# Spiking recommender scores on one core: four more table parts held before the score stage, an opening in two-part chunks, and a plainer last step

## The chip, the cores and the metric

The kernel runs on one core of a Trainium2 chip. The metric is device time in microseconds (us), the median over several executions; one further execution was profiled. Engines are named as in the profile: PE is TensorE (matmul; PEld is its weight load), DVE is VectorE, ACT is ScalarE, POOL is GpSimd, SP is SyncE, which here only issues DMAs. A line such as L478 is a line of the kernel before.

## The reference

```
B, T, D, N = 1024, 50, 128, 100001
e      = emb[seq]                        # row 0 of the table is zero
prefix = cumsum(e, axis=1)
uF     = prefix / minimum(t + 1, lengths)
y      = (uF - mean(uF)) * rsqrt(var(uF) + 1e-5) * gamma + beta    # over the batch, per step
for t in range(T):                       # integrate and fire
    v = v + (y[:, t] - v) / 2
    spike[t] = v >= 1
    v = v - spike[t]
scores = spike.mean(over t) @ emb.T      # 1024 x 100001, f32
```

The inputs are 1024 sequences of 50 indices, their lengths, a table of 100001 rows of 128 f32 values (51 MB), gamma and beta. The output has 409.6 MB.

## The kernel before

**Step stage.** Everything is held with D = 128 on the partitions and the batch of 1024 along the free axis. For each of the 50 steps POOL issues eight indirect DMAs (`gather`, 128 table rows each) into a tile `e`; PE transposes the eight blocks of 128 rows and adds them into two PSUM tiles `pre`, which so hold the running sum. DVE scales them into `uF` and takes the batch statistics (`bn_stats`, `bn_aggr`), ACT takes the square root and centres `uF`, DVE makes the factor `a` out of a few 128x1 operations, ACT writes `x` into the PSUM tile `v`, and DVE applies the old state (`negv`, which is spike minus v) in `step`. PE sums the spikes of every step into `sums` (`counted`). After the last step the spike counts lie in `countA`, `countB` and `countC`, for 128, 512 and 384 of the batch.

In the last step the kernel before cuts the batch into three pieces instead of two halves. The block of 128 that is gathered last (`order.append(order.pop(NB // 2))`) is a piece of its own, so that only a 128-wide `uF` and a 128-wide `bn_stats` follow the last gather. `negv` is formed in three parts (`negated`, `thirds`), placed between the operations of the chain.

**Table parts.** The table is cut into 98 parts of 1024 rows (512 KB each; the last has 673 rows). A part passes through three places. `fetch` brings its rows into a slot of a tile `rows` (six parts to a tile, 24 KB per partition). `prepare` transposes them on PE (eight transposes into PSUM), ACT rounds them to `hi`, DVE subtracts to get `lo`; this pair (8 KB per partition) comes from the list `free`. `product` multiplies a pair with one block of 128 counts: four matmuls of 512 columns per part and block.

36 parts (`AHEAD * GROUP`) are fetched by SP at the start of the step stage and stay in SBUF until used. Two of them are split into pairs during the step stage, at t = 42 and t = 46, which leaves their two row slots empty. When the parts of rows0 have been split, its six slots become three more pairs (`places`), and so do those of rows1. rows2 and rows3 later serve as output tiles. Parts from 36 on are fetched by ACT, three at a time, into rows4 and rows5, from chunk MIDDLE on.

**Score stage.** `WIDTHS` lists how many parts each chunk has. For each chunk and each of eight blocks `n` of 128 batch rows, PE makes the products of the chunk's parts, DVE and ACT in turn scale them from PSUM (four tiles of 1024 columns) into an output tile `o`, and SP stores it with one DMA of 128 rows, each as long as the chunk is wide (4 KB for each part). Output tiles come from the list `turns` in rotation. Before, it has four tiles of two parts for chunks 0 to 2, three of three parts for chunks 3 to 6, and three of six parts from chunk 7 on. The pools of the first two phases are closed and their space is used again. While a chunk is computed, `ready` splits the parts of the next one, at blocks 2 to 7, when a pair is free.

| chunks | before | after |
|---|---|---|
| two parts (8 KB rows) | 0 to 2, parts 0 to 5 | 0 to 10, parts 0 to 21 |
| three parts (12 KB rows) | 3 to 6, parts 6 to 17 | none at the start |
| six parts (24 KB rows) | 7 to 18, parts 18 to 89 | 11 to 21, parts 22 to 87 |
| rest | 4, 4 (the last short) | 4, 3, 3 (the last short) |

Order on each engine is program order (`manual_schedule`). SP waits in that order too: for the output tile's evictions, and for the completion semaphore that a store is given. The stores and ACT's fetches share eight such semaphores in turn, and a DMA is issued only when the previous one on its semaphore has landed.

Of the kernel before, what the change touches and what calls it, by code (L numbers as in the profile page):

```python
# [18 lines left out]
ALU = mybir.AluOpType  # L19
# [8 lines left out]
AHEAD = 6  # L28

WIDTHS = [2, 2, 2, 3, 3, 3, 3] + 12 * [6] + [4, 4]  # L30
NARROW, MIDDLE = 3, 7
# [3 lines left out]
def rec_kernel(  # L35
# [19 lines left out]
    embp = ctx.enter_context(tc.tile_pool(name="embT", bufs=1))  # L55

# [25 lines left out]

    def group(g):
        at = g if g < AHEAD else AHEAD - 2 + g % 2
        r = rowp.tile([P, GROUP, HALF], F32, tag=f"rows{at}", name=f"rows_{g}")
        for k in range(GROUP):
            rows[g * GROUP + k] = r[:, k, :]
        return r

    def fetch(r, q, n):  # L90

        engine = nc.sync if q < AHEAD * GROUP else nc.scalar
        k = q % GROUP
# [67 lines left out]
    with ExitStack() as ph:  # L161
# [3 lines left out]
        up = ph.enter_context(tc.tile_pool(name="uF", bufs=2))  # L165
# [13 lines left out]
        for g in range(AHEAD):  # L179
            fetch(group(g), g * GROUP, GROUP)  # L180
# [3 lines left out]
        def gather(t):  # L184
            es[t] = gp.tile([P, B], F32, tag="e", name=f"e_{t}")
            order = list(range(NB))
            if t == T - 1:
                order.append(order.pop(NB // 2))
            for n in order:
                nc.gpsimd.indirect_dma_start(  # L190
                    out=es[t][:, n * P : (n + 1) * P],
                    out_offset=None,
                    in_=table,
                    in_offset=bass.IndirectOffsetOnAxis(ap=idx[:, n, t : t + 1].bitcast(U32), axis=0),
                )
# [84 lines left out]

        thirds = [slice(0, P), slice(P, P + BANK), slice(P + BANK, B)]

        def negated(cs):
            nc.vector.tensor_tensor(negv[:, cs], s[:, cs], v[:, cs], ALU.subtract)

# [6 lines left out]
        for t in range(T):  # L292
# [4 lines left out]
            if last:  # L297
                s = lp.tile([P, B], BF16, tag="s", name=f"s_{t - 1}")
                nc.vector.tensor_single_scalar(s, v, V_TH, ALU.is_ge)
            uF = up.tile([P, B], F32, tag="uF", name=f"uF_{t}")  # L300


            pieces = halves if not last else halves[:1] + [slice(B - 3 * P, B), slice(BANK, BANK + P)]
            bs = sp.tile([P, len(pieces), 6], F32, tag="bs", name=f"bs_{t}")
            for j, cs in enumerate(pieces):
                h = cs.start // BANK
                if last and j == len(pieces) - 1:

                    counted(t - 1, s)
                for c0 in range(cs.start, cs.stop, P):  # L310
                    k = c0 - h * BANK
                    nc.tensor.matmul(  # L312
                        pre[h][:, k : k + P],
                        lhsT=e[:, c0 : c0 + P],
# [6 lines left out]
                nc.vector.scalar_tensor_tensor(  # L321
                    uF[:, cs],
                    rlen[:, cs],
                    1.0 / (t + 1),
                    pre[h][:, cs.start - h * BANK : cs.stop - h * BANK],
                    ALU.max,
                    ALU.mult,
                )
                nc.vector.bn_stats(bs[:, j, :], uF[:, cs])  # L329
            if not last:  # L330
                correct(t + 1, l)
            else:
                count = once.tile([P, B], F32, tag="zT", name="count")
# [8 lines left out]
            ve = sp.tile([P, 1], F32, tag="ve", name=f"ve_{t}")  # L342
            nc.vector.tensor_scalar_add(ve, mv[:, 1:2], BN_EPS)
# [8 lines left out]
            if last:  # L352
                negated(thirds[0])
            nc.vector.reciprocal(r, r)
            q = sp.tile([P, 1], F32, tag="q", name=f"q_{t}")
            nc.vector.scalar_tensor_tensor(q, r, ve, r, ALU.mult, ALU.mult)
# [11 lines left out]
            if not last:  # L368
                vt = vp.tile([P, B], F32, tag=f"v{t % 2}", name=f"v_{t}")
                x(vt, whole)  # L370
                if t:
                    negated(whole)
# [5 lines left out]
                if t in (T - 8, T - 6):  # L378
                    q = (t - T + 8) // 2
                    prepare(q, vp.tile([P, HALF], F32, tag="v1", name=f"pt_{q}"))  # L380

# [3 lines left out]
        warm = vp.tile([P, HALF], F32, tag="v1", name="warm")  # L385
# [3 lines left out]
        groups = list(zip(thirds, (pre[0][:, :P], pre[1], vC), (countA, countB, countC)))  # L389
        negated(thirds[1])  # L390
# [5 lines left out]
        negated(thirds[2])  # L396
# [29 lines left out]
    to_fetch = AHEAD * GROUP  # L426
# [5 lines left out]
    for c, W in enumerate(WIDTHS):  # L432

        if c in (0, NARROW, MIDDLE):
            opening.close()
            where = opening if c < MIDDLE else ctx
            op = where.enter_context(tc.tile_pool(name="o", bufs=1, reuse_waits="tile"))
            if c == 0:
                third = [op.tile([P, HALF], F32R, tag=x, name=x) for x in ("hi2", "lo2")]
                free.append(third)  # L440
                turns = [(op, f"o{k}", 2) for k in range(4)]
            elif c == NARROW:
                assert third in free
                free.remove(third)
                turns = [(op, f"o{k}", 3) for k in (2, 0, 1)]
            else:
                fourth = op.tile([P, 4, HALF], F32R, tag="pairs", name="pairs")
                free.extend((fourth[:, k, :], fourth[:, k + 1, :]) for k in (0, 2))
# [5 lines left out]
        def ready():  # L454
            nonlocal to_split
            if to_split < q2 and free:
# [3 lines left out]
                if to_split in (GROUP, 2 * GROUP):  # L460
                    places(to_split // GROUP - 1)

        for n in range(NB):
# [5 lines left out]
            for q in range(q0, q1):  # L469
# [12 lines left out]
                if n == NB - 1:  # L482
                    free.append(split.pop(q))
# [6 lines left out]
            if n in (1, 4) and c >= MIDDLE and to_fetch < parts:  # L490
                g = to_fetch // GROUP
                if to_fetch % GROUP or to_split >= (g - 1) * GROUP:
                    if to_fetch % GROUP == 0:
                        r = group(g)
# [23 lines left out]
```

## Time and profile before

| what | value |
|---|---|
| median of 4 runs (lowest to highest) | 1575.21 us (1574.97 to 1575.61) |
| the profiled execution | 1575.07 us |
| its span, first to last instruction | 1573.3 us |
| PE, DVE, ACT, POOL busy | 73%, 60%, 40%, 24% of the span |
| mean granted TensorE clock | 0.944 |
| HBM read, written | 77.69 MB, 409.60 MB |
| first store of scores issued | 510.25 us |
| last store of scores issued | 1561.21 us |

The span has two stages. Until 510 us POOL is the busiest engine beside DVE, and the DMA engines are nearly idle but for the first 64 us, when the 36 parts arrive. From 510 us on the DMA engines move 400 GB/s and more. The busy shares of the first table are means over both stages and tell little by themselves.

### The profile page before, as it was taken

The page shows a single profiled execution, that of the slowest core. Times are in us where ns is not written, and L with a number is a line of the kernel's source. Part 1 is how long each engine was busy: PE and PEld are TensorE (multiplying, and loading weights), DVE is VectorE, ACT ScalarE, POOL GpSimd, SP SyncE. Part 2 cuts the span into 40 slices and gives each one's busy share as a digit, 9 for nine tenths or more (in the row PEclk, how much of TensorE's full clock was granted, in tenths as well). Part 3 has the DMA queues.
Part 4 walks back from the last instruction along what each step waited for, and adds up shares of the span by engine and source line. Part 5 has one row for each costly group of instructions (what it writes and reads, how often), then busy time and mean ns, then how long its engine had stood idle before and what let it go on. Part 6 is the DMA issues. An engine that isn't in the chain of part 4 may idle for free.

```text
span 1573.3 us, 12572 instructions
## 1 busy us (share of the span) xinstructions
PE 1144.6 (73%) x4548; PEld 820.2 (52%) x4548; DVE 947.2 (60%) x1165; ACT 630.5 (40%) x700; POOL 378.4 (24%) x406
## 2 busy tenths in 40 slices
PE   4555554555555998899887888788788788888885
PEld 2222222222233776677666666666676666666663
DVE  5777777777777665576555455555455445555453
ACT  2322222222233554465444444444444444444342
POOL 7777777777775000000000000000000000000000
PEclk9999999999975999999999999999999999999898
DMA  9611111111111999999999999999999999999898
GB/s 337 249 52 54 52 54 52 54 52 54 52 54 46 397 410 418 422 393 427 429 427 431 427 429 427 424 417 406 435 414 429 421 420 426 406 427 425 382 427 354
DMA packets 53691, 488.14 MB, mean 310 GB/s; under 512 B 11995, under 2 KB 12796, under 8 KB 32380
## 3 DMA queue, kind: packets, MB, share of 16 engines
q1 hardware_dynamic: 31984, 428.77, 64.9%
q0 software_dynamic: 12800, 26.24, 5.7%
q10 hardware_dynamic: 8844, 32.33, 5.1%
q8 instruction: 36, 0.59, 0.1%
q14 instruction: 27, 0.22, 0.0%
HBM read 77.69 MB, written 409.60 MB: 310 GB/s over the span
## 4 chain that ended last, share of the span: by engine, by line
DMA 54%; POOL 18%; PE 10%; issue 9%; ACT 5%; DVE 3%; DVEq 0%; POOLq 0%; ACTq 0%; SPq 0%
DMA scores<-o 49%; POOL e L190 18%; PE po L149 9%; DMA e<-in_L_rec_emb_table,idx 5%; ACT o L478 4%; DVE o L476 2%; ACT pairs L141 0%; PE pre L312 0%; PE pt L119 0%; DVE s L349 0%; DVE pairs L142 0%; PE sums L267 0%; DMA idx<-in_r_seq 0%; DVE bs L329 0%; DVE uF L321 0%
## 5 line engine op out<-in xcount | busy, mean ns | idle before, releaser
L476 DVE TENSOR_SCALAR o<-po 128x1024 f32<-128x1024 f32 x391 | 464.2, 1221 | 354.5 <-DMA scores<-o 313.6
L478 ACT ACTIVATE o<-po 128x1024 f32<-128x1024 f32 (+1 forms) x391 | 388.1, 1018 | 551.1 <-DMA scores<-o 340.1
L190 POOL DMA_INDIRECT e<-in_L_rec_emb_table,idx x400 | 377.7, 944 | 124.2 <-issue 112.2
L149 PE MATMUL po<-pairs,countB 128*128 128x512 f32 x1168 | 312.1, 413 | 65.7 <-ACT o L478 48.8
L149 PEld LDWEIGHTS po<-pairs,countB 128*128 128x128 f32 x1168 | 224.5, 197 | 129.7 <-ACT o L478 63.3
L149 PE MATMUL po<-pairs,countC 128*128 128x512 f32 x876 | 242.0, 423 | 50.6 <-ACT o L478 50.5
L312 PE MATMUL pre<-ident,e 128*128 128x128 f32 x400 | 148.7, 450 | 145.3 <-DMA e<-in_L_rec_emb_table,idx 145.3
L149 PEld LDWEIGHTS po<-pairs,countC 128*128 128x128 f32 x876 | 171.5, 202 | 97.4 <-ACT o L478 61.6
L312 PEld LDWEIGHTS pre<-ident,e 128*128 128x128 f32 x400 | 79.0, 200 | 234.2 <-DMA e<-in_L_rec_emb_table,idx 209.9
L142 DVE TENSOR_TENSOR pairs<-pt,pairs 128x1024 fp32r<-128x1024 f32 (+1 forms) x73 | 88.4, 1217 | 95.4 <-ACT pairs L141 95.2
L341 ACT ACTIVATE r<-mv,eps 128x1 f32<-128x1 f32 x50 | 14.8, 295 | 301.3 <-DVE mv L337 301.3
L321 DVE SCALAR_TENSOR_TENSOR uF<-rlen,pre 128x512 f32<-128x512 f32 (+1 forms) x101 | 68.5, 678 | 103.6 <-PE pre L312 103.6
L119 PE MATMUL pt<-ident,rows 128*128 128x128 f32 x782 | 110.6, 288 | 6.5 <-ACT o L478 2.7
L119 PEld LDWEIGHTS pt<-ident,rows 128*128 128x128 f32 x782 | 99.9, 151 | 26.8 <-issue 8.9
L267 PE MATMUL sums<-s,ident_h 128*128 128x512 bf16 x98 | 49.6, 608 | 72.1 <-DVE s L349 72.1
L149 PE MATMUL po<-hi,countB 128*128 128x512 f32 x200 | 83.1, 416 | 18.9 <-ACT o L478 14.1
L256 PE MATMUL pre<-zT,l 128*128 128x512 f32 x100 | 77.4, 776 | 19.6 <-DVE uF L321 19.5
L149 PE MATMUL po<-lo,countB 128*128 128x512 f32 x200 | 80.3, 402 | 0.0
L141 ACT CAST pairs<-pt 128x1024 fp32r<-128x1024 f32 (+1 forms) x73 | 73.6, 1008 | 14.5 <-PE pt L119 14.2
L149 PE MATMUL po<-pairs,countA 128*128 128x512 f32 (+1 forms) x292 | 72.8, 393 | 7.5 <-ACT o L478 7.5
L363 ACT ACTIVATE v<-uF,hgb,a 128x1024 f32<-128x1024 f32 x49 | 59.2, 1209 | 42.2 <-DVE a L359 42.2
L149 PE MATMUL po<-hi,countC 128*128 128x512 f32 x150 | 63.5, 424 | 14.8 <-ACT o L478 14.8
(75 smaller groups left out, 824.6 us busy)
## 6 DMA issues: line engine op xcount, KB each, us to landing
scores<-o SPq DMA_DIRECT2D x96, 3072.0 KB, 20.2
scores<-o SPq DMA_DIRECT2D x32, 1536.0 KB, 8.9
rows<-in_L_rec_emb_table ACTq DMA_DIRECT2D x20, 1536.0 KB, 29.7
scores<-o SPq DMA_DIRECT2D x22, 1024.0 KB, 8.0
rows<-in_L_rec_emb_table SPq DMA_DIRECT2D x6, 3072.0 KB, 35.1
scores<-o SPq DMA_DIRECT2D x8, 2048.0 KB, 13.1
scores<-o SPq DMA_DIRECT2D x8, 1872.5 KB, 11.3
e<-in_L_rec_emb_table,idx POOLq DMA_INDIRECT x400, 2.5
```

The costliest lines, as they stand in the source:

```text
L119: nc.tensor.transpose(pt[:, k0 : k0 + kw], r[:kw, k0 : k0 + D], ident[:kw, :kw])
L141: nc.scalar.copy(vh, vp)
L142: nc.vector.tensor_tensor(vl, vp, vh.bitcast(F32), ALU.subtract)
L149: nc.tensor.matmul(po[:, :kw], lhsT=counts[n], rhs=part[:, k0 : k0 + kw], start=j == 0, stop=j == 1,)
L190: nc.gpsimd.indirect_dma_start(out=es[t][:, n * P : (n + 1) * P], out_offset=None, in_=table, in_offset=bass.IndirectOffsetOnAxis(ap=idx[: ...
L256: nc.tensor.matmul(pre[h], lhsT=l, rhs=zT[:, h * BANK : (h + 1) * BANK], start=t == 0, stop=False, skip_group_check=True,)
L267: nc.tensor.matmul(sums[h], lhsT=ident_h, rhs=s[:, h * BANK : (h + 1) * BANK], start=t == 0, stop=t == T - 2, skip_group_check=True,)
L312: nc.tensor.matmul(pre[h][:, k : k + P], lhsT=e[:, c0 : c0 + P], rhs=ident, start=False, stop=last, is_transpose=True, skip_group_check=True,)
L321: nc.vector.scalar_tensor_tensor(uF[:, cs], rlen[:, cs], 1.0 / (t + 1), pre[h][:, cs.start - h * BANK : cs.stop - h * BANK], ALU.max, ALU. ...
L363: nc.scalar.activation(vt, uF[:, cs], AF.Identity, bias=hgb[:, 1:2], scale=a)
L476: nc.vector.tensor_scalar_mul(o[:, h0 : h0 + hw], po[:, :hw], 1.0 / T)
L478: nc.scalar.mul(o[:, h0 : h0 + hw], po[:, :hw], 1.0 / T)
```

## The change

Four things are changed.

- **Two parts in rows that come free.** After the parts 0 and 1 are split at t = 42 and t = 46, SP fetches parts 8 and 9 into their slots (`LATE`). The tile `uF` has one buffer instead of two.
- **Two parts in a tile of their own.** A tile `extra` (8 KB per partition) receives parts 2 and 3. From chunk 1 on it is one of four output tiles of two parts, and from chunk MIDDLE on it holds a pair. Chunk 0 has three output tiles. Altogether 40 parts are held (`HELD`), and ACT fetches 58 parts instead of 62. `slot` tells where a part lies.
- **Two-part chunks up to part 22.** `WIDTHS` as in the table above; the phase of three-part chunks at the start is gone. The extra pair `third` is taken out of use when 16 parts are split. Chunk 10 has two parts and splits the six parts of chunk 11.
- **The last step in halves.** Its gathers come in the usual order, the batch is taken in two halves, `negv` is formed in one operation ahead of `uF`, and the spike count of step 48 follows the last transposes. In all steps `ve` is gone: the factor takes one more 128x1 operation (`tensor_mul`) after the reciprocal.

```diff
-WIDTHS = [2, 2, 2, 3, 3, 3, 3] + 12 * [6] + [4, 4]
-NARROW, MIDDLE = 3, 7
+LATE = 2
+EXTRA = 2
+HELD = AHEAD * GROUP + LATE + EXTRA
+
+WIDTHS = 11 * [2] + 11 * [6] + [4, 3, 3]
+MIDDLE = 11
...
+    def slot(q):
+        if q < 2 + EXTRA:
+            return 0, q % 2
+        if q < GROUP + EXTRA:
+            return 0, q - EXTRA
+        q -= LATE + EXTRA
+        return max(q, 0) // GROUP, q % GROUP if q >= GROUP else q - GROUP + LATE
...
-        engine = nc.sync if q < AHEAD * GROUP else nc.scalar
-        k = q % GROUP
+        engine = nc.sync if q < HELD else nc.scalar
+        k = slot(q)[1]
...
-        up = ph.enter_context(tc.tile_pool(name="uF", bufs=2))
+        up = ph.enter_context(tc.tile_pool(name="uF", bufs=1))
...
-        for g in range(AHEAD):
-            fetch(group(g), g * GROUP, GROUP)
+        tiles = [group(g) for g in range(AHEAD)]
+        fetch(tiles[0], 0, 2)
+        extra = rowp.tile([P, EXTRA, HALF], F32, tag="extra", name="extra")
+        fetch(extra, 2, EXTRA)
...
+        fetch(tiles[0], 2 + EXTRA, GROUP - 2)
+        for g in range(1, AHEAD):
+            fetch(tiles[g], g * GROUP + LATE + EXTRA, GROUP)
...
-            if t == T - 1:
-                order.append(order.pop(NB // 2))
...
             if last:
                 s = lp.tile([P, B], BF16, tag="s", name=f"s_{t - 1}")
                 nc.vector.tensor_single_scalar(s, v, V_TH, ALU.is_ge)
+                nc.vector.tensor_tensor(negv, s, v, ALU.subtract)
...
-            pieces = halves if not last else halves[:1] + [slice(B - 3 * P, B), slice(BANK, BANK + P)]
...
-                if last and j == len(pieces) - 1:
-                    counted(t - 1, s)
...
             else:
+                counted(t - 1, s)
                 count = once.tile([P, B], F32, tag="zT", name="count")
...
-            ve = sp.tile([P, 1], F32, tag="ve", name=f"ve_{t}")
-            nc.vector.tensor_scalar_add(ve, mv[:, 1:2], BN_EPS)
...
-            if last:
-                negated(thirds[0])
             nc.vector.reciprocal(r, r)
             q = sp.tile([P, 1], F32, tag="q", name=f"q_{t}")
-            nc.vector.scalar_tensor_tensor(q, r, ve, r, ALU.mult, ALU.mult)
+            nc.vector.tensor_mul(q, r, r)
+            nc.vector.scalar_tensor_tensor(q, mv[:, 1:2], BN_EPS, q, ALU.add, ALU.mult)
...
                     prepare(q, vp.tile([P, HALF], F32, tag="v1", name=f"pt_{q}"))
+                    fetch(tiles[0], GROUP + EXTRA + q, 1)
+                    rows[GROUP + EXTRA + q] = tiles[0][:, q, :]
...
-        warm = vp.tile([P, HALF], F32, tag="v1", name="warm")
+        warm = vp.tile([P, HALF], F32, tag="v0", name="warm")
...
-        negated(thirds[1])
...
-        negated(thirds[2])
...
-    to_fetch = AHEAD * GROUP
+    to_fetch = HELD
...
-        if c in (0, NARROW, MIDDLE):
+        if c in (0, 1, MIDDLE):
             if c == 0:
+                op = opening.enter_context(tc.tile_pool(name="o", bufs=1, reuse_waits="tile"))
...
-                turns = [(op, f"o{k}", 2) for k in range(4)]
-            elif c == NARROW:
-                assert third in free
-                free.remove(third)
-                turns = [(op, f"o{k}", 3) for k in (2, 0, 1)]
+                turns = [(op, f"o{k}", 2) for k in range(3)]
+            elif c == 1:
+                turns = [(rowp, "extra", 2)] + turns
             else:
-                fourth = op.tile([P, 4, HALF], F32R, tag="pairs", name="pairs")
-                free.extend((fourth[:, k, :], fourth[:, k + 1, :]) for k in (0, 2))
+                assert third not in free and third not in split.values()
+                opening.close()
+                op = ctx.enter_context(tc.tile_pool(name="o", bufs=1, reuse_waits="tile"))
+                for pool, tag in ((op, "pair"), (rowp, "extra")):
+                    t = pool.tile([P, 2, HALF], F32R, tag=tag, name=f"pair_{tag}")
+                    free.append((t[:, 0, :], t[:, 1, :]))
                 turns = [(rowp, "rows2", 6), (rowp, "rows3", 6), (op, "o", 6)]
             blocks = 0
...
-                if to_split in (GROUP, 2 * GROUP):
+                if to_split in (GROUP + LATE + EXTRA, 2 * GROUP + LATE + EXTRA):
                     places(to_split // GROUP - 1)
+                    if to_split > 2 * GROUP and third in free:
+                        free.remove(third)
...
-                    free.append(split.pop(q))
+                    pair = split.pop(q)
+                    if pair is not third or to_split < 2 * GROUP + LATE + EXTRA:
+                        free.append(pair)
                     ready()
...
-                g = to_fetch // GROUP
-                if to_fetch % GROUP or to_split >= (g - 1) * GROUP:
-                    if to_fetch % GROUP == 0:
+                g, k = slot(to_fetch)
+                if k or to_split >= (g - 1) * GROUP + LATE + EXTRA:
+                    if k == 0:
```

## The prediction

> **What bounds the kernel now.** I read the page's slices first. In its DMA line the DMA engines are idle while the steps run and full from the fourteenth slice on, where PE is at 8 to 9 tenths: two stages with different limits.
>
> ```profile
> PE   4555554555555998899887888788788788888885
> ...
> DMA  9611111111111999999999999999999999999898
> ...
> DMA 54%; POOL 18%; PE 10%; issue 9%; ACT 5%; DVE 3%; DVEq 0%; POOLq 0%; ACTq 0%; SPq 0%
> ```
>
> The third line is the chain of work that ended last: POOL with its gathers for the steps, then DMA with the stores. So a saving in the score stage counts if it takes bytes or gaps from the DMA engines, and one in the steps only if the last gather is followed sooner. The second view is the table of windows over the score stage (length, busy time of PE, PEld, DVE, ACT, POOL, then PE clock, DMA share, GB/s).
>
> ```profile
> 525.00:565.00 40.00, 37.11 (x176) 28.58 (x174) 26.39 (x22) 21.92 (x22) 0.00 (x0) 1.00 1.01 418
> 565.00:580.00 15.00, 12.11 (x49) 9.32 (x48) 7.26 (x6) 5.78 (x6) 0.00 (x0) 0.89 0.97 403
> 580.00:660.00 80.00, 71.23 (x328) 54.65 (x327) 47.25 (x40) 39.61 (x41) 0.00 (x0) 1.00 1.00 419
> 660.00:690.00 30.00, 27.22 (x136) 20.81 (x134) 19.46 (x17) 17.20 (x18) 0.00 (x0) 1.00 0.99 415
> 690.00:700.00 10.00, 9.62 (x42) 7.99 (x43) 7.95 (x8) 5.46 (x6) 0.00 (x0) 1.00 0.82 343
> ...
> 760.00:1440.00 680.00, 559.80 (x2431) 440.75 (x2432) 359.26 (x304) 299.41 (x304) 0.00 (x0) 0.93 1.00 423
> ...
> 1460.00:1480.00 20.00, 17.12 (x71) 13.48 (x70) 8.97 (x9) 8.22 (x9) 0.00 (x0) 0.91 0.79 336
> 1480.00:1560.00 80.00, 63.27 (x273) 48.98 (x271) 40.77 (x38) 31.71 (x36) 0.00 (x0) 0.96 1.01 425
> ```
>
> The share is 1.0 in all but three: two-part chunks (first row) move 418 GB/s, three-part 419, six-part with fetches 423. The gaps are the passage to three parts (565 to 580), that to six (690 to 700), and one at 1460 to 1480. The third view, SP's waits from 1430 to 1490 (total, times, longest), names the last; the page's DMA issues have the fetch it waits for.
>
> ```profile
> SPq L158 <- DMA rows<-in_L_rec_emb_table: 14.1, 1, 14.1
> ```
>
> ```profile
> rows<-in_L_rec_emb_table ACTq DMA_DIRECT2D x1, 320.0 KB, 46.7
> ```
>
> A store had the same completion semaphore as the 320 KB fetch of the last part (issued at 1428.8, 46.7 us to landing) and waited for it. Fourth, the timeline at the last step:
>
> ```profile
> 498.96 1.21 DVE L284 TENSOR_TENSOR negv<-s,v 128x1024 f32<-128x1024 bf16 x1
> ...
> 501.64 1.22 DVE L299 TENSOR_SCALAR s<-v 128x1024 bf16<-128x1024 f32 x1
> ...
> 502.78 0.68 DVE L321 SCALAR_TENSOR_TENSOR uF<-rlen,pre 128x512 f32<-128x512 f32 x1
> 503.50 0.69 DVE L329 BATCH_NORM_STATS2 bs<-uF 128x6 f32<-128x512 f32 x1
> ...
> 505.33 0.29 DVE L321 SCALAR_TENSOR_TENSOR uF<-rlen,pre 128x128 f32<-128x128 f32 x1
> 505.65 0.29 DVE L329 BATCH_NORM_STATS2 bs<-uF 128x6 f32<-128x128 f32 x1
> 505.98 0.24 DVE L337 BATCH_NORM_AGGREGATE mv<-bs 128x2 f32<-128x18 f32 x1
> ```
>
> The last gather lands at about 504.7; behind it come only the 128-wide pair and the aggregate, done at 506.22. The rest of the chain leads to the first store at 510.25.
>
> **The change part by part.** The sum is made against the profiled execution, 1575.07 us (span 1573.3 and 1.8 around it), 0.14 under the median of 1575.21.
>
> *Fewer reads in the full stage.* Four parts of 0.524 MB, 2.10 MB, leave a stage that moves 423 GB/s: 2.10 / 0.423 = 4.96 us. **-4.96.** Their reading goes where DMA has room: parts 2 and 3 lengthen the first fetch by 1.05 MB at the 388 GB/s of 20 to 60 us (2.7 us), parts 8 and 9 come at t = 42 and 46, where 52 GB/s flow. In both POOL issues its 16 to 17 gathers in 20 us, with or without the fetch beside them, so I cost this at nothing. SP has nothing queued behind the two late fetches until the stores. If the cover failed, two gathers would land later by up to 1.3 us each (0.52 MB at 400 GB/s), four steps before the end, where DVE still waits 2.2 us a step for the last transposes.
>
> *Shorter rows.* 22 parts go out in two-part chunks instead of 6. Twelve of the sixteen replace three-part chunks; the stretch of 580 to 690 as a whole also moved 418, so these are even. Four replace six-part chunks: 16.8 MB at 418 instead of 423, +0.5. At the end 5.66 parts, 23.7 MB, go out in three-part rows at 419 instead of 425: +0.8. **+1.3.** The packet records give an upper bound: 317 ns for 8192 bytes, 469 for 12288, 924 for 24576, 619 for 16384; over 16 engines that is 10.13, 10.00, 9.86 and 9.90 us a part, in all 969.8 instead of 966.7 us, +3.1. A lower bound comes from completions: two-part stores landed 2.50 us apart (10.0 a part), three-part ones 3.84 (10.24), so twelve parts would gain 2.9, in all -1.6. [...]
>
> *No passage to three parts.* 565 to 580 moved 403 instead of 418: 15 x (1 - 403/418) = 0.54. **-0.5.**
>
> *The passage to six parts.* Before it cost 10 x (1 - 343/419) = 1.8 us: a six-part block needs 6 x 4 matmuls at 0.227 us apart, 5.45 us, before its store goes out. After, chunk 10 splits six parts beside two-part blocks. A block with a split takes PE 8 x 0.227 + 0.87 = 2.7 us, its store 2.5: 0.2 lost in each of six blocks, about 1 us, half of it covered by PE's lead in four PSUM tiles. DVE (1.22 + 1.23) just keeps up. From the landing that frees the output tile, the first six-part store needs an eviction (1.2), five products (4.6) and the last eviction (1.2), 7 us; stores in line cover 8.6 (issue to landing of a two-part store) less 1.6 of fixed latency, also 7. So some 1 us of gap is left. **-0.8**, bounds -1.8 (no gap) and +2.8 (PE at the 0.91 clock of many slices: 2.97 us a block, 2.8 lost, on top of today's gap).
>
> *The last step.* `negv` (1.21) now stands between `s`, which ends at 502.86, and `uF`: first half 504.1 to 505.5, second half (0.69 + 0.69, transposes done at 505.3) to 506.95, aggregate to 507.2, against 506.22: +0.95. The extra 128x1 operation costs 0.19 with its gap; 0.1 of it hides behind ACT's centring, which ended at 507.58 against 507.50 for `a`. **+1.05**, bounds 0.7 and 1.6. The spike count moves behind the last transposes on PE; ACT's copies of it then end near 506.9, just before the square root. In the other 49 steps the same operation lies under the 2.2 us wait: nothing. One `uF` buffer adds no wait: DVE writes `uF` only after its own `step`, which already waits for ACT's `x`.
>
> *Three output tiles in chunk 0.* Its sixth block must wait for a store that landed at 525.7 and is issued at about 527 instead of 524.7; then chunk 1 reuses o0 after one block. The queue then holds two stores and nearly covers it. **+0.4**, bounds 0 and 1.5. Behind the waiting evictions on DVE and ACT stand the next evictions, and PE stops when its four PSUM tiles are full.
>
> *The gap at 1460 to 1480.* Worth 20 x (1 - 336/425) = 4.2 us for the mean engine. But the slowest completions run on through it (1472.0, 1479.5, 1487.0, 1494.4: 7.5 apart, as elsewhere), so the engine that ends last lost nothing. After, the last part is fetched three blocks later in its chunk. **0**, bounds -3.9 and +6. [...]
>
> Sum: -4.96 + 1.3 - 0.5 - 0.8 + 1.05 + 0.4 = -3.5 us: 1571.5.
>
> **The rivals.**
> - *Two-part rows cost their packets, and the passage stays as dear.* Terms +3.1 and 0 instead of +1.3 and -0.8: 1574.1. For it: the packet means. Against it: 418 in both stretches.
> - *PE is the bound in chunk 10.* Passage +2.8 instead of -0.8: 1575.1. For it: PE has 37.1 of 40 us already with two splits a chunk. Against it: its clock was 1.00 there.
> - *Slower: the shared semaphore, longer.* The store after the last fetch would stand among four-part stores, which come 5.1 us apart instead of 7.7. If it is again the sixth, it is due 0.6 + 3 x 7.7 + 2 x 5.1 = 34 us after the fetch and waits 13 instead of 7: +6, 1577.5, up to 1580. It decides once the wait exceeds the stores in line, about 9 us. [...]
> - *The gap at 1460 goes and counts in full:* -3.9, 1567.6.
> - *The four parts' reads cost nothing before*, so nothing is gained. Against it: DMA share 1.00 beside them. I give it no chance of its own.
>
> **How the numbers follow.** Forecast 0.52 (own range 1569.3 to 1573.5), dear rows 0.14, PE-bound 0.10, longer wait 0.14, gap gone 0.10. A measurement here tells about 0.2%, 3.15 us, from no change: faster is under 1572.06, slower over 1578.36. Faster: 0.7 of 0.52, and 0.10, with a little of dear rows, 0.47. Slower: half the longer wait and some of PE-bound, 0.11. Same: 0.42. The range, 1567.0 to 1577.8, reaches from the gap gone to the longer wait.
>
> **What would show it.** Right: HBM read still 77.69 MB, but ACT's fetches fewer by four parts; the first store near 511.3; 418 GB/s to about 735 us; no dip near 573; a dip of at most 2 us at the passage near 735. Wrong: a rate under 412 in the two-part chunks, a dip of 4 us at 735, a wait of SP for `rows` over 10 us near the end, or a first store off 511.3 by more than 0.5.

## The result, and the profile after

The changed kernel takes 1577.18 us (40 runs, 1576.52 to 1578.18), the kernel before 1575.22 (60 runs): ratio 1.0013 [1.0009, 1.0017]. The change costs 2.0 us where 3.5 were to be gained. The profiled execution took 1577.47 us, its span 1575.6.

The page of the changed kernel, DMA and GB/s by slice, and the chain that ended last:

```profile
DMA  9711111111121999999999999999999999999998
GB/s 341 271 53 52 54 52 53 52 54 53 53 80 45 368 416 417 413 406 372 427 425 431 428 426 426 427 426 422 421 419 427 428 421 426 412 408 429 410 387 361
DMA 55%; POOL 17%; PE 12%; issue 7%; ACT 4%; DVE 3%; ACTq 0%; DVEq 0%; POOLq 0%; SPq 0%
```

The two stages and their limits are as they were. The 80 in the twelfth slice is the late fetch of parts 8 and 9. From the fifteenth slice to the eighteenth the two-part chunks run at 416 to 406 GB/s, falling. The windows say it by stage (columns as in the prediction's table, the last three being PE clock, DMA share and GB/s):

```profile
525.00:565.00 40.00, 33.88 (x158) 26.12 (x156) 23.24 (x20) 19.73 (x20) 0.00 (x0) 1.00 0.95 390
565.00:580.00 15.00, 12.92 (x61) 9.71 (x60) 9.01 (x9) 7.94 (x9) 0.00 (x0) 1.00 1.01 417
580.00:660.00 80.00, 70.64 (x313) 51.58 (x312) 46.11 (x40) 37.79 (x39) 0.00 (x0) 1.00 1.01 416
660.00:690.00 30.00, 26.81 (x121) 19.79 (x120) 18.98 (x16) 15.67 (x16) 0.00 (x0) 1.00 0.99 406
735.00:745.00 10.00, 9.75 (x45) 7.73 (x44) 8.19 (x7) 5.80 (x6) 0.00 (x0) 1.00 0.65 265
760.00:1440.00 680.00, 564.28 (x2454) 444.35 (x2453) 362.16 (x308) 303.08 (x308) 0.00 (x0) 0.93 1.00 424
1460.00:1480.00 20.00, 14.88 (x57) 11.27 (x56) 7.07 (x6) 6.83 (x7) 0.00 (x0) 0.83 0.93 395
```

Four things stand here. The first row, 418 at a share of 1.01 before, has a hole: 390 at 0.95. The dip at 565 to 580 is gone. The two-part chunks move 416 to 417 at a share of 1.01 up to 660 us, near the prediction's 418, and 406 at 0.99 behind it; their packets of 8192 bytes keep a mean of 316 to 318 ns in all of it, so what slows them late is not the mean packet (e3 below). The passage to six parts, now at 735, shows the mean engine idle for a third of 10 us.

Every store leaves 16 completions in the trace. I count it as done at the last of them, and the engine that is last can differ from the mean (2.60 us a store against 2.51 in e3 below). So I also cut the score stage by those last completions:

```
us, by last completions             before            after    difference  predicted
first store issued                  510.25           510.93          +0.7      +1.05
to the 21st store's landing           48.1             50.8          +2.7      +0.4
rest of the opening                  140.5            183.7   +43.2
  (4 parts more)                                     - 39.9          +3.2       0.0
six-part chunks                      795.6            731.2   -64.4
  (6 parts fewer)                                    + 59.9          -4.5      -5.8
the last chunks                       77.8             98.0   +20.2
  (2 parts more)                                     - 20.0          +0.3      +0.8
sum                                                                  +2.4      -3.5
```

The sum is that of the two profiled executions (1577.47 and 1575.07 us). A part is taken at 9.99 us, 8/6 of the 7.49 between the landings of the last six-part stores of before (1471.97, 1479.54, 1487.01, 1494.44). The predicted column groups the prediction's own terms: the opening has +0.5 of the shorter rows and the passage to three parts, the six-part row the reads and the other passage. Two rows, the second and the third, miss by 5.5 of the 5.9 us, and the experiments are about these.

In some of the later runs (e5, e5b, e6, e8, f0 to f3 and h2 below) the step stage was some 70 us longer for every kernel, that of before too, so those times near 1650 are read only as ratios to the kernel before in the same session, or by the score stage alone: first store issued to last landing, 1062.0 us for before and 1063.8 after.

### The profile page after: what moved, and what is told of

The parts are those of the page before. It is cut to its first block, busy times and chain, and to the rows that moved or that the text cites. A ratio compares the mean times of both kernels' runs of the same rounds, so it can differ in the third digit from the quotient of the medians.

```text
span 1575.6 us, 12744 instructions
## 1 busy us (share of the span) xinstructions
PE 1156.7 (73%) x4548; PEld 815.8 (52%) x4548; DVE 942.2 (60%) x1161; ACT 633.2 (40%) x700; POOL 378.3 (24%) x406
## 4 chain that ended last, share of the span: by engine, by line
DMA 55%; POOL 17%; PE 12%; issue 7%; ACT 4%; DVE 3%; ACTq 0%; DVEq 0%; POOLq 0%; SPq 0%
DMA scores<-o 49%; POOL e L207 17%; PE po L162 11%; DMA e<-in_L_rec_emb_table,idx 6%; ACT o L481 4%; DVE o L479 2%; PE pt L132 1%; PE pre L316 0%; DVE s L346 0%; DVE bs L326 0%; DVE uF L325 0%; DMA idx<-in_r_seq 0%; PE sums L284 0%; ACTq L481 0%; PE sums L162 0%
## 5 line engine op out<-in xcount | busy, mean ns | idle before, releaser
L481 ACT ACTIVATE o<-po 128x1024 f32<-128x1024 f32 x391 | 391.3, 1022 | 554.7 <-DMA scores<-o 336.8
L162 PE MATMUL po<-pairs,countB 128*128 128x512 f32 (+1 forms) x880 | 236.2, 416 | 52.4 <-ACT o L481 41.1
L162 PEld LDWEIGHTS po<-pairs,countB 128*128 128x128 f32 x880 | 167.6, 197 | 105.8 <-ACT o L481 57.3
L162 PE MATMUL po<-pairs,countC 128*128 128x512 f32 x660 | 181.9, 424 | 35.8 <-ACT o L481 35.6
L162 PEld LDWEIGHTS po<-pairs,countC 128*128 128x128 f32 x660 | 129.1, 203 | 73.2 <-ACT o L481 46.6
L325 DVE SCALAR_TENSOR_TENSOR uF<-rlen,pre 128x512 f32<-128x512 f32 x100 | 68.4, 684 | 108.0 <-PE pre L316 108.0
L162 PE MATMUL po<-hi,countB 128*128 128x512 f32 x232 | 96.7, 417 | 19.2 <-ACT o L481 14.1
L155 DVE TENSOR_TENSOR pairs<-pt,pairs 128x1024 fp32r<-128x1024 f32 (+1 forms) x55 | 66.4, 1216 | 61.1 <-ACT pairs L154 61.1
L326 DVE BATCH_NORM_STATS2 bs<-uF 128x6 f32<-128x512 f32 x100 | 69.5, 695 | 3.5
L162 PE MATMUL po<-lo,countC 128*128 128x512 f32 x174 | 69.3, 398 | 0.0
```

Of the source, the lines that this page charges most:

```text
L155: nc.vector.tensor_tensor(vl, vp, vh.bitcast(F32), ALU.subtract)
L162: nc.tensor.matmul(po[:, :kw], lhsT=counts[n], rhs=part[:, k0 : k0 + kw], start=j == 0, stop=j == 1,)
L325: nc.vector.scalar_tensor_tensor(uF[:, cs], rlen[:, cs], 1.0 / (t + 1), pre[h], ALU.max, ALU.mult)
L326: nc.vector.bn_stats(bs[:, h, :], uF[:, cs])
L481: nc.scalar.mul(o[:, h0 : h0 + hw], po[:, :hw], 1.0 / T)
```

## The experiments

**The last step as before** (e1).

```diff
...
-            for h, cs in enumerate(halves):
+            for j, cs in enumerate(pieces):      # 512, 384, 128; negv in thirds; ve
...
```

> The changed kernel with the last step of the kernel before (three pieces, parted negv, ve). Theory (the slowest DMA engine sets the end; what precedes the first store adds to it one for one): first store back from 510.93 to about 510.25, time 0.7 below the changed kernel, 1576.5. Rival (the score stage starts slowly enough to hide it): no difference, 1577.2.

1576.88, ratio 1.0009 [0.9999, 1.0018]. The last step takes little back: the medians differ by 0.3, less than the intervals can separate, and the first store went out at 510.77. Over all profiled runs with the shorter step stage the first store went out at 510.93 to 511.64 with the changed last step (six kernels, mean 511.3) and at 510.25 to 510.77 with the old one (five, mean 510.5). In the timelines of the last step (start, duration, line) the changed kernel has

```profile
502.61 1.22 DVE L311 TENSOR_TENSOR negv<-s,v 128x1024 f32<-128x1024 bf16 x1
503.75 0.68 DVE L325 SCALAR_TENSOR_TENSOR uF<-rlen,pre 128x512 f32<-128x512 f32 x1
505.08 0.67 DVE L325 SCALAR_TENSOR_TENSOR uF<-rlen,pre 128x512 f32<-128x512 f32 x1
505.78 0.69 DVE L326 BATCH_NORM_STATS2 bs<-uF 128x6 f32<-128x512 f32 x1
506.51 0.21 DVE L336 BATCH_NORM_AGGREGATE mv<-bs 128x2 f32<-128x12 f32 x1
...
510.93 0.84 SPq L171 DMA_DIRECT2D scores<-o  x2
```

and e1 has

```profile
506.27 0.24 DVE L357 BATCH_NORM_AGGREGATE mv<-bs 128x2 f32<-128x18 f32 x1
```

The aggregate ends 0.2 to 0.5 us later in halves (506.72 against 506.51 and, in the kernel before, 506.22), where 0.95 was predicted: `uF` started at 503.75, as `negv` ended (503.83 by the timeline), where the prediction had 504.1.

**Chunk 1's output tiles in another turn** (e2), so that chunk 1 does not reuse o0 one block after `extra`.

```diff
-                turns = [(rowp, "extra", 2)] + turns
+                turns = [(rowp, "extra", 2)] + turns[1:] + turns[:1]
```

> The changed kernel, but chunk 1 takes its output tiles in the order extra, o1, o2, o0, so that o0, used last in chunk 0, is used again last. Theory: the wait at 534 to 538 goes, and of the 2.7 us that chunks 0 and 1 lose some 1.5 to 2.2 come back: 1575.0 to 1575.7. Rival (the loss is chunk 0's three tiles, not the order): under 0.5 back, 1576.7 or more.

1576.50, ratio 1.0008 [0.9999, 1.0017]; score stage 1061.8, which is 1.9 less than after. The time fell by only 0.7, which lies between the two expectations and inside the intervals: the first store of the profiled execution went out 0.7 us later, at 511.64. The windows of the changed kernel,

```profile
525.00:535.00 10.00, 6.85 (x32) 4.96 (x31) 4.71 (x4) 3.98 (x4) 0.00 (x0) 1.00 0.93 383
535.00:540.00 5.00, 3.45 (x21) 2.66 (x19) 2.36 (x2) 2.67 (x3) 0.00 (x0) 1.00 0.66 272
```

and of e2,

```profile
525.00:535.00 10.00, 7.09 (x33) 5.21 (x32) 5.41 (x5) 3.98 (x4) 0.00 (x0) 1.00 0.97 401
535.00:540.00 5.00, 5.00 (x28) 4.22 (x27) 2.71 (x3) 3.18 (x4) 0.00 (x0) 1.00 0.98 403
```

show the second part of the hole and its end: PE stood for 1.5 of 5 us and now does not. In the changed kernel the stores were issued nearly 5 us and over 4 us apart there (523.70, 528.35; 534.02, 538.37). Two waits for output tiles stand behind this. The store of 528.35 waited for the tile of three blocks before, whose store landed at 526.94; e2 keeps that wait. The store of 538.37 waited for o0, whose store landed at 536.96; that one e2 takes away. To the landing of the 21st store the nine profiled runs with the change's tiles and turns took 50.2 to 51.6 us, e2 and the two mended runs below 48.4 to 49.3, and the kernels with four tiles in chunk 0 48.0 to 48.7.

**The two-part opening alone, in the kernel before** (e3): no part more is held.

```diff
-WIDTHS = [2, 2, 2, 3, 3, 3, 3] + 12 * [6] + [4, 4]
+WIDTHS = 9 * [2] + 12 * [6] + [4, 4]
...
```

> The kernel before with its first 18 parts in nine two-part chunks (36 parts held, its four two-part output tiles kept to chunk 9). Theory (the slowest engine needs 10.37 us a part in two-part rows, 10.24 in three-part rows): 12 parts x 0.13 = 1.6 more, and 0.8 more at the passage to six parts: 1577.6. Rival, as the prediction had it (two- and three-part rows even at 418 GB/s, one passage fewer): 0.5 less, 1574.7.

1577.37, ratio 1.0013 [1.0004, 1.0022]: as slow as the whole change, without its reads, its tiles and its last step. The windows of before had 418 in all of 580 to 690 and 343 at 690 to 700. Here:

```profile
580.00:690.00 110.00, 97.19 (x442) 71.77 (x441) 65.72 (x55) 54.90 (x56) 0.00 (x0) 1.00 1.00 411
690.00:700.00 10.00, 9.75 (x47) 7.75 (x46) 8.21 (x8) 5.73 (x6) 0.00 (x0) 1.00 0.64 262
620.00:640.00 20.00, 17.44 (x78) 12.63 (x77) 11.48 (x10) 9.26 (x11) 0.00 (x0) 1.00 1.01 417
660.00:680.00 20.00, 17.45 (x75) 12.50 (x74) 11.28 (x11) 9.65 (x10) 0.00 (x0) 1.00 0.99 408
```

The 411 is a mean of two stretches: 416 to 417 up to 640 us, and 408 to 409 from 640 to 680, with some engines idle. By last completions the eight stores of chunk 1 and those of chunk 2 took 20.05 us, and every later eight 20.7 to 20.9, from about 585 us on, while the mean engine still ran at 417. The 16 completions of each store, as lags behind their median, show what changed:

```
e3, store                               13    17    21    25    31    32    41    49    53
completion that falls back, us        0.50  0.86  1.22  1.60  2.16  2.80  3.57  4.25  4.61
last of the others, us                2.57  2.59  2.55  2.56  2.55  2.56  2.50  2.48  2.45
```

One completion falls back by 0.09 us with every two-part store, and by 0.6 us once, at the 32nd; its engine so takes 2.60 us a store where the median takes 2.51. (The records do not name the engine; that it is one and the same is read from the even growth.) Up to the 31st store another engine, with a constant lag, comes last, and the landings are 2.50 us apart; then the falling one passes it and the landings are 2.60 apart. When its lag has reached 4.8 us (55th store, 647 us) it hardly grows further (4.6 to 5.0) and the other engines stand idle in part, which is the 408. The kernel before has only 28 stores up to the end of its two-part chunks: its falling completion was then 1.84 us behind, and another, at 2.17, was still last. Why one engine is slower is not shown. The passage looks worse in the windows (262), but its first six-part store landed 7.6 us after the last two-part one, as in before: that gap is one of the mean engine.

**The last fetch in long rows** (e4). The 640 rows of the last part are fetched in pieces of 2560 bytes; its columns come out in another order.

```diff
-                    in_=table[c1 : c1 + full * P, :].rearrange("(k p) d -> p k d", p=P),
+                    in_=table[c1 : c1 + full * P, :].rearrange("(p k) d -> p k d", p=P),
```

> The kernel before, but the 640 whole rows of the last part are fetched in 128 pieces of 2560 bytes instead of 640 of 512 (the columns of that part so come out in another order). The store then finds its semaphore free and the gap at 1470 goes. Theory (the slowest engine runs on through that gap): no difference, 1575.2. Rival (the gap costs what the mean engine loses): 3.9 less, 1571.3.

1575.69, ratio 1.0002 [0.9993, 1.0011]. The fetch (page, DMA issues) and the window of the gap:

```profile
rows<-in_L_rec_emb_table ACTq DMA_DIRECT2D x1, 320.0 KB, 21.0
```

```profile
1460.00:1480.00 20.00, 17.33 (x73) 13.55 (x72) 9.83 (x9) 7.87 (x8) 0.00 (x0) 0.91 1.01 431
```

It landed in 21.0 us instead of 46.7, and the gap is gone, 431 instead of 336 GB/s, with nothing gained. Each engine had 32 small packets fewer to pass and the fetch landed 25.7 us sooner, 0.8 us for each, as if each small packet had waited for nearly one 24 KB packet (0.92 us). The gap of the mean engine was no loss here; in before the last completions ran on through it, 7.5 us apart.

**Two parts held, without the opening** (e5, then with a wide tail, e5b).

```diff
...
+LATE, EXTRA = 2, 0
-WIDTHS = [2, 2, 2, 3, 3, 3, 3] + 12 * [6] + [4, 4]
+WIDTHS = 4 * [2] + 4 * [3] + 12 * [6] + [3, 3]      # e5
+WIDTHS = 4 * [2] + 4 * [3] + 13 * [6]               # e5b
```

> The kernel before with only the two late parts (38 held, in the rows that come free): chunks 4 x 2, 4 x 3, 12 x 6, 3, 3; no tile extra, four output tiles in chunk 0, the last step of the kernel before. Theory (each held part saves its 1.3 us of reading, the loss is in the opening): reading -2.6, two more parts in the opening +0.5, tail -0.3: 1572.9 where the kernel before has 1575.3. Rival (the reads cost nothing before): 1575.5 or more.

> As the last, but the tail is a thirteenth six-part chunk (its last part short) in place of 3, 3. Theory (the slowest engine sets the end: 5.66 parts at 9.96 instead of 57.6 us in three-part rows): 1.3 less, 1571.6. Rival (a wide last store ends later after its last product, by half of its 7.5 us): 1575 or more.

0.9985 [0.9974, 0.9997] and 0.9987 [0.9978, 0.9995], score stages 1061.1 and 1059.7. The same two kernels again:

> The kernel before with two late parts held, opening 4 x 2 and 4 x 3, tail 3, 3, on another chip than at first. Theory: 1061.1 us from the first store to the last landing as measured there, so 1.0 below the kernel before: 1574.3. Rival (reads cost nothing): 1575.5.

> The same with a thirteenth six-part chunk at the end. Theory: 1059.7 us of score stage, 2.4 below the kernel before: 1572.9. Rival (the wide last store costs at the end): no better than with the narrow tail, 1574.3.

0.9996 [0.9987, 1.0005] and 0.9988 [0.9979, 0.9997], stages 1060.6 and 1059.9. Two held parts with the wide tail so take 2.1 to 2.5 us from the score stage (g2 below included). That the reads pay is seen without the tail: e5 and f1 have as many six-part stores as before, 96, and took 793.6 and 793.7 us for them, against 795.6 in before and 795.8 and 796.1 in e3 and e4, which read all 62 parts.

**The change, mended** (e8, and again as f3): e1 and e2 together, and a tail of six and four parts. Beside f3 ran the change itself once more (f0).

```diff
-WIDTHS = 11 * [2] + 11 * [6] + [4, 3, 3]
+WIDTHS = 11 * [2] + 12 * [6] + [4]
```

> The changed kernel with the last step of the kernel before, chunk 1 taking extra, o1, o2, o0, and a tail of a twelfth six-part chunk and one of four parts. Theory: 1577.2 - 0.5 - 1.5 - 1.2 = 1574.0, under the kernel before by about 1.2; the two-part opening (2.0 measured alone) is what keeps it from more. Rival (the losses overlap): 1575.5 or more.

> The changed kernel with the last step of before, the rotated turns and the tail 6, 4. Theory: 1061.2 us of score stage: 0.9 below the kernel before, 1574.4, and 2.9 below the changed kernel. Rival (last step and turns overlap): 1575.5.

> The changed kernel as it is, beside the others on one chip. 2.0 above the kernel before where the step stage runs at full clock, and 1063.8 us from the first store's issue to the last landing (before: 1062.1).

0.9995 [0.9986, 1.0003] and 0.9993 [0.9983, 1.0003], stages 1061.2 and 1060.3; f0 1.0023 [1.0014, 1.0032], 1064.2. Mended, the change no longer loses, but with four parts held it is not ahead of two held in wider rows. Its 96 six-part stores took 791.4 and 791.3 us, with four reads fewer than before.

**Every six-part store as three of two parts** (e6).

```diff
-                store(n, q0 * HALF, o[:, : min(N, q1 * HALF) - q0 * HALF])
+                for h0 in range(0, min(N, q1 * HALF) - q0 * HALF, 2 * HALF):
+                    store(n, q0 * HALF + h0, ...)
```

> The changed kernel, every six-part store issued as three stores of two parts (8 KB rows), nothing else changed: 66 parts in 8 KB rows. Theory (10.37 us a part on the slowest engine instead of 9.96): 66 x 0.41 = 27 more than the changed kernel, 1604. Rival 1 (packet means, 10.13 instead of 9.86): 18 more, 1595. Rival 2 (rates of windows, 418 instead of 423 GB/s): 8 more, 1585. Rival 3 (the slower opening has to do with its place and not with its rows): none, 1577.

Ratio 1.0157 [1.0139, 1.0175], score stage 1090.3: 26.5 more, as the theory had it, for 200 further stores (24 of them from the last chunks), 0.13 us each. The window 760 to 1440, here all in 8 KB rows, moved 408 GB/s for 424:

```profile
760.00:1440.00 680.00, 562.32 (x2446) 444.13 (x2445) 363.03 (x306) 302.68 (x306) 0.00 (x0) 0.92 1.00 408
```

That left open whether the rows' length or the stores' number costs. Two runs meant for it gave no answer.

**Four stores of 32 full rows** (g1).

```diff
...
+                for p0 in range(0, P, P // 4):
+                    nc.sync.dma_start(out=out[r0 + p0 : ...], in_=o[p0 : p0 + P // 4, :w])
```

> The changed kernel, each six-part store issued as four stores of 32 batch rows with full 24 KB rows: 352 stores instead of 88, rows as long as before. Theory (the slowest engine pays by the length of its rows): score stage 1063.8 us as in the changed kernel. Rival (it pays about 0.1 us for each store, however long its rows, as its lag in two-part chunks grows by 0.1 a store): 264 more stores, +26 us, 1090.

2079.36, ratio 1.3202 [1.3179, 1.3226]; neither expectation was near. From 800 to 1900 us:

```profile
800.00:1900.00 1100.00, 646.96 (x2333) 505.17 (x2331) 346.62 (x291) 287.80 (x292) 0.00 (x0) 0.76 0.91 249
```

Packets of the same 24 KB took 1490 ns in the mean (median 1653) for 922 (median 912).

**Two stores with 8 KB rows** (h2): parts 0, 1, 4, 5 in the one, 2 and 3 in the other.

> The changed kernel with each six-part store issued as two stores whose rows are 8 KB pieces (parts 0, 1, 4 and 5 in the one, parts 2 and 3 in the other): 176 stores in place of 88, with the same bytes and the same 128 partitions. Three such stores gave a score stage of 1090.3 us against 1063.8. Theory (the slowest engine pays by the length of the row): the rows are as short as with three stores, so the same loss, a score stage of about 1090 us and a time of about 1603. Rival (each store costs about 0.1 us whatever its rows): 88 more stores, about 9 us, a score stage of 1073 and a time of 1586.

Ratio 1.1055 [1.103, 1.108]. SP's waits (total, times, longest) say why it tells nothing of rows:

```profile
SPq L495 <- DMA scores<-o: 824.9, 88, 14.0
```

The two stores' column ranges overlap, though no element does, and SP waited 88 times, as often as there are pairs, for a store to land.

**One store with shorter rows** (h3, h4): the number of stores stays, the six-part chunks are taken in pairs, and a row goes out as three pieces of 8 KB, or six of 4 KB, to every other place of the pair's columns, which so stand in another order.

```diff
...
+                to = out[n * P : (n + 1) * P, b0 * HALF : (b0 + 2 * GROUP) * HALF].rearrange(
+                    "p (j two w) -> p j two w", two=2, w=2 * HALF)      # h4: w=HALF
+                nc.sync.dma_start(out=to[:, :, odd, :], in_=src)
```

> The changed kernel; ten of its eleven six-part chunks are taken in pairs, and the three 8 KB pieces of each row go to every other 8 KB place of the pair's columns, so that each store is still one DMA of 3 MB and 128 rows, but each row is written as three rows of 8 KB. The columns of those chunks stand in another order. The number of stores stays at 88 of six parts. The run with two stores had its second store wait for the first to land (824.9 us in 88 waits), so it told nothing. Theory (the slowest engine pays about 0.15 us for every 128 further rows, whether they come in a store of their own or not: 26.5 us for the 176 further stores of the run with three): 160 further sets of rows, 24 us, a score stage of 1088 and a time of 1601 at the full clock, ratio 1.0167 to before. Rival (each store costs, its rows do not): 1064 and 1577, ratio 1.0013.

> As the kernel with 8 KB rows in one store, but with six rows of 4 KB for each row, to every other 4 KB place of the pair's columns; the columns of those chunks stand in another order. Theory (0.15 us for every 128 further rows): 400 further sets of rows, 60 us, a score stage of 1124 and a time of 1637 at the full clock, ratio 1.039. Rival (each store costs, its rows do not): 1064 and 1577, ratio 1.0013.

Ratios 1.0112 [1.0095, 1.0129] and 1.0307 [1.029, 1.0324]; score stages 1079.3 and 1113.6, 15.5 and 49.8 over after. The windows of h3, then of h4:

```profile
760.00:1440.00 680.00, 559.24 (x2402) 442.32 (x2401) 354.53 (x301) 297.31 (x300) 0.00 (x0) 0.92 1.01 415
```

```profile
760.00:1440.00 680.00, 546.15 (x2279) 431.53 (x2276) 335.89 (x284) 281.68 (x286) 0.00 (x0) 0.89 1.02 395
```

The rival (rows are free) falls. The theory's sign is right, its size too large: 128 further rows cost 15.5 / 160 = 0.10 us and 49.8 / 400 = 0.12, not 0.15. The packet records give most of it: 8192 bytes took 317 ns, 10 more than a third of 922; 4096 bytes 169, 15 more than a sixth. At eight rows per engine that is 0.08 and 0.12 us. The rates of these windows, 415 and 395 GB/s, are 2.1% and 6.8% under the 424 of the changed kernel.

**Two stores of 64 full rows** (k1): even partitions in the one, odd in the other; the rows of a block stand in another order in these columns.

```diff
...
+                for k in range(2):
+                    nc.sync.dma_start(out=out[r0 : r0 + P // 2, ...], in_=o[k:P:2, : 6 * HALF])
```

> The changed kernel with each six-part store issued as two stores of 64 rows of 24 KB, the even partitions of the output tile in the one and the odd ones in the other; the rows of each block of 128 stand in another order in those columns. 176 stores in place of 88, the same number of rows and the same row length. One store with three rows of 8 KB for one of 24 cost 0.10 us for every 128 further rows (score stage 1079.2 for 1063.8), six rows of 4 KB 0.125 (1113.6). Theory (the rows cost, their stores hardly): at most what the run with three stores has over that, (26.5 - 200 x 0.10) / 200 = 0.03 us a store, 3 us: a score stage of 1064 to 1067 and a time of 1577 to 1580 at the full speed of the steps. Rival (a store costs 0.15 us whatever its rows): 88 x 0.15 = 13, 1077 and 1590. The run with four stores of 32 neighbouring partitions moved 249 GB/s; if it was the few rows of a store that were slow there, stores of 64 rows should be slow too, between 249 and 424 GB/s, some 340, a stage of about 1200; if it was that the rows lay in neighbouring partitions, these run at 424. [...]

1606.6, ratio 1.0201 [1.0184, 1.0218]; score stage 1090.7. The window and SP's waits:

```profile
760.00:1440.00 680.00, 542.36 (x2362) 428.10 (x2361) 348.49 (x296) 291.90 (x296) 0.00 (x0) 0.92 0.96 406
```

```profile
SPq L494 <- DMA rows<-in_L_rec_emb_table: 236.5, 15, 18.0
```

Both expectations for the price of a store miss. The engines are idle for 4% of 680 us, 27 us, as much as the stage grew, and SP waited 15 times, up to 18 us, for a fetch. Stores and fetches share eight completion semaphores (eight in the traces of before and after), and with twice the stores a semaphore that a fetch holds comes round twice as soon. That these waits made the idle time is argued, not shown: e6 had such waits too (215.3 us in 20), but its engines stayed at a share of 1.00 beside them. What a store costs beside its rows stays open. The packets took 923 ns, as in the changed kernel: 64 rows to a store are not slower than 128 when they lie on every second partition. That leaves the neighbouring partitions as the likely cause in g1; 32 rows in another layout were not tried.

**The version that beats both** (g2): e5b once more, here beside a kernel before with the shorter step stage.

> Two late parts held, opening 4 x 2 and 4 x 3, thirteen six-part chunks, for a time at full clock if this chip grants it. Score stage 1059.8 us, 2.2 below the kernel before: 1573.0 where that has 1575.2. Rival (the gain belongs to the slow step stage of the other chips): 1575.2.

1572.84 beside 1575.12 for before, ratio 0.9985 [0.9976, 0.9994]; score stage 1059.5. Against after's 1.0013 the intervals do not meet.

## Why the prediction was wrong

**Shorter rows: the step that failed.** The prediction took +1.3 between -1.6 and +3.1; the opening and the last chunks cost +3.2 and +0.3 by last completions, 3.5, of which the passage to three parts that went may hide some. It priced rows by GB/s, and the mean engine did run at 415 to 418 up to 660 us, near the foreseen 418; but the stage ends with its slowest engine, which takes 2.60 us for a two-part store and not the 2.50 of the prediction's lower bound. Both rows that it read, the 418 GB/s of 525 to 565 and the 2.50 us between landings, come from the first 28 stores, in which another engine was still last (e3). Over the rest of the opening it was 183.7 / 71 = 2.587, or 10.35 us a part. In the prediction's own terms, "these are even" is what failed: by last completions two-part rows cost 10.4 us a part, three-part rows 10.2 and six-part rows 10.0. e3 shows the term alone: 2.0 us by the medians, 1.8 by the score stage, with 16 further sets of 128 rows (23 chunks for 21). After has 25 chunks, 4 x 8 = 32 further sets; at the 0.10 us of h3 that is 3.2. The packet means, held as an upper bound (+3.1), came near, though the mean engine was not what set the pace.

**Three output tiles in chunk 0: mis-sized.** +0.4 was taken of 0 to 1.5; it was about +2.7, and e2, which only turns the tiles, gets 1.9 of that back. The prediction named the place and said that the queue would nearly cover it. It did not: two waits left the mean engine idle for some 0.5 us in 530 to 535 and 1.7 in 535 to 540, and PE stood behind them.

**The reads: right.** The six-part stores of e8 and f3, as many as before and with four reads fewer, took 4.5 us less than those of before, e3 and e4 in the mean, though their first landing came 0.9 us later behind the last two-part one; e5 and f1, with two reads fewer, took 2.2 less. That is 1.1 to 1.4 us a part, so the four reads gave 4.4 to 5.4 of the predicted 5.0.

**The passages.** No dip is left at 565 to 580, as foreseen, but that -0.5 was a gap of the mean engine: in before the first three-part store landed 3.7 us after the last two-part one, no more than its own 3.84. At 735 the dip is some 10 x (1 - 265/405) = 3.5 us of the 405 GB/s ahead of it, against at most 2 foreseen, and the first six-part store landed 8.3 us after the last two-part one, 7.6 in before: +0.7 where -0.8 was taken, inside the bounds. The PE-bound rival (+2.8) has its dip but not its price. The 1.6 us of fixed latency in the prediction's estimate is near what the four 256 KB stores of before give: 2.2 us from issue to landing, less 0.63 at 418 GB/s, an estimate.

**The last step: right in sign and nearly in size,** +0.7 for +1.05; first issues of the same step differ by up to 0.7 between runs, and the means of all runs are 0.8 apart.

**The gap at 1460: right.** SP's waits in the changed kernel, and the fetch:

```profile
SPq L171 <- DMA rows<-in_L_rec_emb_table: 10.4, 1, 10.4
```

```profile
rows<-in_L_rec_emb_table ACTq DMA_DIRECT2D x1, 320.0 KB, 38.8
```

The wait is still there, 10.4 us for 14.1, and the last completions run through it (1469.1, 1476.6, 1481.7, 1486.8). The prediction's sign of being wrong, a wait over 10 us, came and cost nothing; before had 14.1 already. The slower rival's 1577.5 came near the time by another cause: its longer wait did not happen, so that the time lies in the range, whose upper end stood for that wait, is luck. Nor would removing the gap have paid, as e4 shows; its price, worked out as 4.2 us and carried on as 3.9, was 0.

In sum, the places were named and the gain of the reads was there, but two costs taken at 1.3 and 0.4 us were 3.5 and 2.7, the first because the pace was taken from the mean engine and from the first stores.

## What to carry to other kernels

In a stage that the DMA engines fill, price a change of shape by the last of each store's 16 completions over a long stretch, until it is the slowest engine that comes last, and not by GB/s over the first tens of microseconds or by the gaps of the mean engine. A held part saved 1.1 to 1.4 us here, and that was a gain only where the chunks stayed wide and the rotation of output tiles as deep; two parts held (0.9985 to 0.9988 with the wide tail) did better than the four of this change (1.0013, mended 0.9993 and 0.9995) because they cost less of both. When a store is cut to test something, look first at what else the cut changes: the partitions it reads (249 GB/s in g1), the ranges it overlaps (824.9 us of waits in h2) and the semaphores it uses up (236.5 us of waits in k1).

## What the runs showed of the hardware that was not expected

Stores of 32 neighbouring partitions moved 249 GB/s (g1), stores of every second partition kept packets of 923 ns (k1), with the same 24 KB rows. In g1 many packets took near twice the 912 ns of the changed kernel's median (upper quartile 1908); why is not shown.

One of a store's 16 completions fell back by 0.09 us with every two-part store (e3), so that the engine that set the pace was seen as the last only after 31 stores.

In f0, whose step stage was longer, POOL's waits have a row that the changed kernel's own profile lacks:

```profile
POOL e L207 <- remote: 64.4, 16, 4.4
```

Gathers stood 16 times for some 4 us behind something that the trace does not record. It does not belong to the chip: h2 has the same row (67.9 us in 17), while h3 and h4, on the same chip some minutes later, have none. The granted clock alone is not the cause: in 150 to 350 us it was 0.50 in g2 and h3, which have no such row and issued their first stores at 510.3 and 511.55, and 0.53 in f0. The cause stays open.
